# Weighting both halves of the first states with C in one product, and adding the residual inside the output projection

## The chip, the cores and the metric

The kernel runs on one core of a Trainium2 chip. The metric is the device time of one execution in microseconds; "the time" of a kernel is the median of several runs. Five engines work from queues of their own: TensorE (PE in the profile, with its weight loads as PEld), VectorE (DVE), ScalarE (ACT), GpSimd (POOL) and SyncE (SP), which issues nearly all the DMAs.

## The reference, cut to what matters

One decoder layer on x of shape (4, 512, 256): a two-layer state-space (Mamba-like) block, cross attention, and a mixture-of-experts block, each with a residual. Only the first matters here:

```
x = x + ssm(layernorm(x))          # ssm keeps a residual stream of its own, cur
for l in 0, 1:
    cur = cur + block(rmsnorm(cur))

block: xb, z   = split(in_w @ .)              xb = silu(conv(xb))
       delta, B, C = projections of xb        delta = softplus(...)
       dA[e,n,t] = exp(delta[e,t] * A[e,n])   mi[e,n,t] = delta[e,t] * B[n,t] * xb[e,t]
       v[t] = 0.6 * v[t-1] + mi[t]            h[t] = dA[t] * h[t-1] + v[t]      (16 states n, 512 channels e)
       y[e,t] = sum_n h[e,n,t] * C[n,t] + D[e] * xb[e,t]
       return out_w @ (y * silu(z))
```

So each of the 4 x 2 = 8 (layer, batch) steps ends in an output projection of 512 tokens x 256 features, whose result is added to `cur`; after layer 1 the layer's own input x is added as well.

## The kernel before, in words

The stage runs over eight steps s = (l, b): layer 0 with batches 0 to 3, then layer 1. A step has eight pairs (lines 652 and on): a pair is one block of 128 channels (e, four of them) and two of its four groups q of 32 channels. The 128 partitions of a tile hold 32 channels times four states. A pair has state slots n = 0 to 3. For n = 1, 2, 3 one whole unit each treats both groups in tiles of 128 x (2 x 512). For n = 0, the first states, there are two half units of 128 x 512, one for each group j. The five units of a pair come in an order written by hand (`TURNS`, line 59; f is a whole unit, h a half): "ffhfh" for the first four pairs, "fhfhf" for three, "hfhff" for the last. In all there are 192 whole and 128 half units. A unit's number within the step is its slot, 0 to 39.

A whole unit: POOL makes `m` = dx * B (`driven`, line 693), two whole units ahead; DVE scans it with 0.6 into `v` (L729, in PSUM) and then with the decay into `h` (L738); POOL weights `h` with C in place (`weighted`, L751); PE sums over the states into the PSUM tile `y` with the matrix `joined` (`summed`, L765). A half unit has no `m` and no first scan: PE filters by a banded matrix into the PSUM tile `vf` (`filtered`, L711, 20 small products, placed two units ahead; the pool holds one `vf`), and DVE scans that with the decay into `hh` (L726). POOL weights each half when it has been scanned. The two halves of a pair go to PE together:

```
hc = weighted(u, h)
...
pending.append((u, hc[:, 0, :], hc[:, 1, :]) if n > 0 else (u, half, hc[:, 0, :]))
```

Decays are made by ScalarE with Exp (`decayed`, L684), three groups ahead, into four tiles. Once the units of a channel block are done, `finished` (L778) multiplies `y` with the gate `z` on DVE. After the last block of a step, it starts `projected`, a generator that advances one piece at each whole unit of the next step. Its first piece runs at slot 3 of that step, the second at slot 5, the end at slot 6. A piece computes 256 tokens with eight matmuls into a PSUM tile `po` of 128 x 2 x 256 (L798), from the pool "mm" of two buffers, which all products of the background share:

```
for t in range(0, TB, 2):
    po = ps.tile([P, 2, D], F32, tag="mm", name="po")
    ...
    yield
    cur = xs[:, b, t : t + 2, :]
    nc.vector.tensor_tensor(cur, cur, po, ALU.add)
    if l == NL - 1:
        nc.gpsimd.tensor_tensor(cur, cur, xt[:, t : t + 2, :], ALU.add)
```

`xs` in SBUF holds the residual stream `cur` of all four batches. Layer 1 loads x again into `xt` by a DMA on SP at the head of its projection (L793). The last step's projection isn't made here but in the attention stage (L1343), by code of its own. So seven projections pass through `projected`: four of layer 0, three of layer 1.

Beside this, a background generator, `prologue`, prepares the next step (norm, transposes `pt` L474, `xnT` L477, input products `pp` L383, convolution `pc` L490, softplus through `sum` L572, DMAs to and from HBM), with the current step's gates in between (product L383, Silu L465). It rests while a projection is under way, except at slots 1 to 4. [...] At slot 2 PE has `vf` for slot 4, the first product of a new `y` (L761) and the sums held back; at slot 3 the first `po`; at slot 4 a gate product `pp` and a sum; at slot 5 the second `po` and then `vf` for slot 7.

Of the kernel before, what the change touches and what calls it, by code (L numbers as in the profile page):

```python
# [10 lines left out]
F32 = mybir.dt.float32  # L11
I32 = mybir.dt.int32
AF = mybir.ActivationFunctionType
ALU = mybir.AluOpType
# [3 lines left out]
P = 128  # L18
B, L, D = 4, 512, 256
KD = D // P  # L20
TB = L // P
NL = 2
# [45 lines left out]
def decoder_layer(  # L68
# [26 lines left out]
    nc = tc.nc  # L95
# [5 lines left out]
    xs = const.tile([P, B, TB, D], F32, name="xs")  # L101

    ident = const.tile([P, P], F32, name="ident")
# [106 lines left out]
    with ExitStack() as ph:  # L210
# [7 lines left out]
        pre6 = ph.enter_context(tc.tile_pool(name="ssm_pre6", bufs=6))  # L218
        ring2 = ph.enter_context(tc.tile_pool(name="ssm_ring2", bufs=2))
        ring3 = ph.enter_context(tc.tile_pool(name="ssm_ring3", bufs=3))  # L220
        ps_beta = ph.enter_context(tc.tile_pool(name="ssm_ps_beta", bufs=1, space=PSUM))
        ps_v = ph.enter_context(tc.tile_pool(name="ssm_ps_v", bufs=1, space=PSUM))
        ps_vf = ph.enter_context(tc.tile_pool(name="ssm_ps_vf", bufs=1, space=PSUM))
# [430 lines left out]
        for i in range(len(pairs)):  # L654
            ns, js = iter(range(1, SQ)), iter(((0,), (1,)))
# [42 lines left out]
        left = []  # L698

        filtering = {}  # L700

        def filtered(u):

# [16 lines left out]
        def scanned(u):  # L720
            i, n, js = units[u]
            dA = decaying[i, n][:, js[0] : js[-1] + 1, :]
            if n == 0:
                v = filtering.pop(u)
                h = ring3.tile([P, L], F32, name="hh")
                nc.vector.tensor_tensor_scan(h, dA[:, 0, :], v, 0.0, ALU.mult, ALU.add)  # L726
                return h.unsqueeze(1)
            v = ps_v.tile([P, 2, L], F32, name="v")
            nc.vector.tensor_tensor_scan(  # L729
                v.rearrange("p n t -> p (n t)"),  # L730
                beta.rearrange("p n t -> p (n t)"),
                entering.pop(u).rearrange("p n t -> p (n t)"),
                0.0,
                ALU.mult,
                ALU.add,
            )
            h = ring3.tile([P, 2, L], F32, name="h")
            nc.vector.tensor_tensor_scan(  # L738
                h.rearrange("p n t -> p (n t)"),
                dA.rearrange("p n t -> p (n t)"),  # L740
                v.rearrange("p n t -> p (n t)"),
                0.0,
                ALU.mult,
                ALU.add,
            )
            return h

        def weighted(u, h):
            i, n, js = units[u]
            Cs = made[pairs[i][0]][3][1]  # L750
            nc.gpsimd.tensor_tensor(h, h, Cs[n].unsqueeze(1).to_broadcast([P, len(js), L]), ALU.mult)  # L751
            return h

        def summed(u, *hcs):
# [32 lines left out]
        def projected(s, z):  # L787

            l, b = s
            outw = weights[l][5][0]  # L790
            if l == NL - 1:
                xt = pre1.tile([P, TB, D], F32, tag="w", name="xt")
                nc.sync.dma_start(xt, blocks(x[b]))  # L793
            for t in range(0, TB, 2):
                po = ps.tile([P, 2, D], F32, tag="mm", name="po")
                for i in range(2):
                    for k in range(NE):
                        nc.tensor.matmul(  # L798
                            po[:, i, :],
                            z[k // 2][:, k % 2, (t + i) * P : (t + i + 1) * P],  # L800
                            outw[:, k, :],
                            start=(k == 0),
                            stop=(k == NE - 1),
                        )
                yield
                cur = xs[:, b, t : t + 2, :]
                nc.vector.tensor_tensor(cur, cur, po, ALU.add)
                if l == NL - 1:
                    nc.gpsimd.tensor_tensor(cur, cur, xt[:, t : t + 2, :], ALU.add)


        DOUBLE = (8, 23, 38), (8, 13, 18, 23, 30, 33, 38)
# [23 lines left out]
        pending = []  # L836
# [74 lines left out]
        for u, (i, n, js) in enumerate(units):  # L911
            s, e, q = pairs[i]
            if u % 16 == 15 and empty < NX * ROWS + SPARE * P:
                empty = emptied(empty)
            if u % 16 == 7:
                next(fillers, None)
            if u % per == 0 and (e, q) == (0, 0):
                k = steps.index(s)
                if k == 0:
                    background = chained(background, prologue(*steps[1], s))  # L920
                    foreground = None
                else:
                    for _ in background:
                        pass
                    if s == (1, 0):
                        load_others(1)
                    if k + 1 < len(steps):
                        background, foreground = prologue(*steps[k + 1], s), None
                    else:
                        background, foreground = kept_from(), gates(s)  # L930

                fetching = k > 0 and k + 1 < len(steps) and steps[k + 1][0] == 0
                if fetching:
                    next(background)
                slot = 0
            if s == (1, 0) and slot == 10:
                load_last(1)
            if u in groups and groups.index(u) + LEAD < len(groups):
                later = groups[groups.index(u) + LEAD]
                i2 = units[later][0]  # L940
                if later % per == 0 and i2 + 1 < len(pairs):
                    while pairs[i2 + 1] not in stored:
                        next(background)
                    copied(i2 + 1)
                owed.append(later)
            between = units[u - 1][1:] == (0, (0,))
            while owed and not between and (n > 0 or 0 in js):
                decayed(owed.pop())
            if n > 0 and wholes.index(u) + AHEAD < len(wholes):
                driven(wholes[wholes.index(u) + AHEAD])  # L950
            gating = 3 if TURNS[i // 2 * 2 % len(TURNS)][1] == "h" else 2
            if u % per == gating and q == 0 and u > per:
                finished(*pairs[i - 1][:2])
            h = scanned(u)
            if projections:

                if n > 0 and next(projections[0], s) is s:
                    projections.pop()
            elif slot > 1 and foreground is not None:
                if next(foreground, s) is s:  # L960
                    foreground = None
            early = n == 0 and js == (0,)
            hc = weighted(u, h)

            def filters():
                if u + 2 < len(units) and units[u + 2][1] == 0:
                    s2, e2 = pairs[units[u + 2][0]][:2]
                    while (s2, e2 // 2) not in ready:
                        next(background)
                    filtered(u + 2)  # L970

            def sums():

                while pending and not 0 < slot % (2 * per) < gating:
                    summed(*pending.pop(0))

            if early:
                filters()
                sums()
                half = hc[:, 0, :]  # L980
            else:
                if n > 0:
                    filters()
                if 0 < slot <= 4 or not projections and foreground is None and not (fetching and slot == 0):
                    held = next(background, None)
                    if held is None and not projections and (
                        n > 0 and (k == 0 and slot < 20 or k == len(steps) - 1 or units[(u + 1) % len(units)][1] > 0) or slot in DOUBLE[k < len(steps) - 1]
                    ):
                        next(background, None)
                if n == 0:  # L990
                    filters()
                sums()
                pending.append((u, hc[:, 0, :], hc[:, 1, :]) if n > 0 else (u, half, hc[:, 0, :]))
            if k + 1 < len(steps) and slot in (36, 38):
                spread(steps[k + 1], 0 if slot == 36 else 3)
            if slot == 36 and k + 1 < len(steps):
                bands = banded()
            if slot >= 36 and k + 1 < len(steps):
                for _ in range(2):
                    next(bands, None)  # L1000
            slot += 1
# [263 lines left out]
    with ExitStack() as ph:  # L1265
# [20 lines left out]
        for i in range(2):  # L1286

            t = wp.tile([P, TB, P], F32, name=f"tops{i}")
# [10 lines left out]
        xt = ring.tile([P, TB, D], F32, tag="wide", name="xt")  # L1299
# [74 lines left out]
        n = B * NG * 8  # L1374
        for s in range(-LEAD, n + 2):
            u, k = divmod(s, 8)
            kb, hp = divmod(k, 2)
            b, g = divmod(u, NG)
# [340 lines left out]
```

## Time and profile before

| | us |
|---|---|
| median of 3 runs (1794.42 to 1799.02) | 1794.95 |
| the profiled execution, its own time | 1799.32 |
| its span, first to last instruction | 1797.6 |
| mean granted TensorE clock | 0.935 |

The groups of instructions that the change removes, merges or adds to (by line, with shapes kept apart; xN is the count, then the busy time in us and the mean ns of one):

| line, engine, what | count | busy us | mean ns |
|---|---|---|---|
| L751 POOL, `h` times C, 128x1024 | 192 | 452.6 | 2357 |
| L751 POOL, `hh` times C, 128x512 | 128 | 163.0 | 1274 |
| L807 DVE, `xs` plus `po`, 128x512 | 14 | 9.6 | 683 |
| L809 POOL, `xs` plus `xt`, 128x512 | 6 | 7.6 | 1269 |
| L798 PE, `po`, 128x256 | 224 | 52.1 | 386 |
| L484 ACT, copy from PSUM, 128x512 | 32 | 18.6 | 581 |

L798 counts two instructions for each matmul of this data type (112 matmuls). Matmuls overlap, so the mean of one is longer than its pace: 16 in a row take 3.72 us. The page gives each engine's busy share, and its busy tenths in 40 slices of 45 us; the state-space stage is slices 2 to 27. The waits view says who waited for whom. The chain of waits goes back from the last instruction, at each step to what released it. A timeline row holds the start, the duration, the engine, line, operation and tiles, and in square brackets the idle time before it with what ended it.

### The profile page before, as it was taken

How to read it: one execution, taken by the hardware profiler on the slowest of the kernel's cores; microseconds unless marked ns; L12 is line 12 of the kernel's file. 1: busy time of each engine (PE TensorE's matmuls, PEld its weight loads, DVE VectorE, ACT ScalarE, POOL GpSimd, SP SyncE). 2: the span in 40 equal slices, each digit the busy share in tenths (PEclk: the TensorE clock that was granted, in tenths of full speed). 3: DMA queues.
4: the chain of work that ended last, by engine and by line, in shares of the span. 5: the costliest groups of instructions: out<-in, count | busy, mean ns of one | idle time of the engine just before them, and what ended most of it. 6: DMA issues, size and time to landing. Idle time of an engine off the chain costs nothing.

```text
span 1797.6 us, 28225 instructions
## 1 busy us (share of the span) xinstructions
PE 1569.9 (87%) x10682; PEld 737.0 (41%) x10682; DVE 1379.8 (77%) x1252; ACT 1027.8 (57%) x1613; POOL 1242.0 (69%) x781
## 2 busy tenths in 40 slices
PE   7779789879879879879879978987999999889998
PEld 3333344334334334334424324433233333466665
DVE  1498899989999999999999998995567676532223
ACT  3758767747876866866776865541444444412221
POOL 4588999989989999999999999992000202245540
PEclk9889999989999889989979988996999999999999
DMA  2543543553553653634553443533310100442214
GB/s 64 142 106 92 138 109 98 121 112 95 132 131 78 151 132 99 155 100 101 140 133 83 138 114 99 161 109 120 106 59 24 59 1 24 145 119 66 65 59 152
DMA packets 122991, 185.71 MB, mean 103 GB/s; under 512 B 19464, under 2 KB 58248, under 8 KB 122856
## 3 DMA queue, kind: packets, MB, share of 16 engines
q1 hardware_dynamic: 117576, 169.45, 36.0%
q0 software_dynamic: 5280, 14.46, 2.6%
q8 instruction: 85, 1.39, 0.3%
q14 instruction: 50, 0.41, 0.1%
HBM read 124.38 MB, written 59.46 MB: 102 GB/s over the span
## 4 chain that ended last, share of the span: by engine, by line
PE 60%; DVE 16%; ACT 11%; issue 7%; POOL 3%; DMA 3%; SPq 0%; DVEq 0%; POOLq 0%; ACTq 0%
DVE v L729 7%; PE y L765 7%; PE pc L490 6%; PE sT L1415 6%; PE pp L383 5%; PE vf L711 5%; DVE h L738 4%; PE pu L1569 4%; PE pw L1592 4%; PE o L1328 3%; ACT decay L684 3%; PE sum L572 3%; PE sc L1415 3%; PE po L798 2%; PE y L761 2%
## 5 line engine op out<-in xcount | busy, mean ns | idle before, releaser
L751 POOL TENSOR_TENSOR h<-h,Cs 128x1024 f32<-128x1024 f32 x192 | 452.6, 2357 | 49.6 <-DVE h L738 39.9
L693 POOL TENSOR_TENSOR m<-dxs,Bs 128x1024 f32<-128x1024 f32 x192 | 452.8, 2359 | 16.1 <-DMA deltas<-wide 16.1
L738 DVE TENSOR_TENSOR_SCAN h<-decay,v 128x1024 f32<-128x1024 f32 x192 | 439.0, 2286 | 17.0 <-DVE v L729 0.5
L729 DVE TENSOR_TENSOR_SCAN v<-beta,m 128x1024 f32<-128x1024 f32 x192 | 437.9, 2281 | 14.8 <-POOL m L693 9.8
L684 ACT ACTIVATE decay<-deltas,scaleA 128x511 f32<-128x511 f32 x512 | 332.0, 712 | 58.5 <-DVE h L738 57.4
L711 PE MATMUL vf<-band,dxT 106*32 106x102 f32 (+1 forms) x5120 | 184.5, 269 | 87.3 <-DVE hh L726 86.5
L765 PE MATMUL y<-h,joined 128*32 128x512 f32 x768 | 210.3, 643 | 30.3 <-POOL h L751 30.0
L1421 DVE TENSOR_REDUCE tops<-sc 128x2 f32<-128x1024 f32 x128 | 156.3, 1225 | 96.5 <-PE sc L1415 96.3
L711 PEld LDWEIGHTS vf<-band,dxT 106*32 106x32 f32 (+1 forms) x5120 | 145.6, 117 | 165.6 <-issue 109.8
L1426 ACT ACTIVATE at<-sT 128x1024 f32<-128x1024 f32 x128 | 128.8, 1024 | 140.6 <-PE sc L1415 109.0
L726 DVE TENSOR_TENSOR_SCAN hh<-decay,vf 128x512 f32<-128x512 f32 x128 | 154.1, 1204 | 31.0 <-PE vf L711 31.0
L751 POOL TENSOR_TENSOR hh<-hh,Cs 128x512 f32<-128x512 f32 x128 | 163.0, 1274 | 13.8 <-DVE hh L726 10.2
L113 POOL TENSOR_TENSOR rstd<-ve,neghalf 128x4 f32<-128x4 f32 x12 | 12.3, 1027 | 204.3 <-DVE ve L111 204.3
L1415 PE MATMUL sc<-kpad,qpad 32*128 32x512 f32 x512 | 146.1, 668 | 7.2 <-ACT at L1426 4.8
L1415 PE MATMUL sT<-q,kpad 32*128 32x512 f32 x512 | 139.4, 658 | 3.3 <-DVE q L1320 3.3
L383 PE MATMUL pp<-xnT,inw 128*128 128x512 f32 x256 | 124.0, 622 | 4.9 <-ACT z L649 3.4
L490 PE MATMUL pc<-xpad,taps 128*128 128x512 f32 x256 | 118.9, 604 | 0.0
L765 PEld LDWEIGHTS y<-h,joined 128*32 128x32 f32 x768 | 35.5, 115 | 141.2 <-issue 67.2
L1601 POOL DMA_INDIRECT rows_out<-yg,target x39 | 40.0, 1027 | 77.1 <-DVE xgT L1562 69.1
L1196 POOL DMA_INDIRECT rows_in<-row,at x32 | 31.8, 994 | 80.8 <-DVE stat L1209 39.6
L684 ACT ACT_TABLE_LOAD x62 | 79.5, 1283 | 4.6 <-DMA deltas<-wide 3.5
L1585 DVE COPY hgT<-pf 128x512 f32<-128x512 f32 x39 | 27.0, 692 | 68.3 <-PE pf L1583 68.3
(252 smaller groups left out, 2301.3 us busy)
## 6 DMA issues: line engine op xcount, KB each, us to landing
dxs<-wide SPq DMA_DIRECT2D x256, 128.0 KB, 2.7
deltas<-wide SPq DMA_DIRECT2D x256, 128.0 KB, 3.1
rows_in<-nothing SPq DMA_DIRECT2D x17, 1028.0 KB, 8.9
Cs<-rows SPq DMA_DIRECT2D x128, 64.0 KB, 3.3
wide<-w SPq DMA_DIRECT2D x16, 512.0 KB, 2.8
wide<-ln SPq DMA_DIRECT2D x16, 512.0 KB, 3.8
Bs<-rows SPq DMA_DIRECT2D x32, 192.0 KB, 3.8
xt<-in_x_dram SPq DMA_DIRECT2D x8, 512.0 KB, 7.2
```

What stands on the lines that cost most here:

```text
L383: nc.tensor.matmul(pp, weights[l][1][half][:, k, m * P : (m + 1) * P], xnT[:, k, :], start=(k == 0), stop=(k == KD - 1),)
L490: nc.tensor.matmul(pcs[j], taps[:, e, k, :], xpads[j][:, k : k + L], start=(k == 0), stop=(k == KC - 1),)
L684: nc.scalar.activation(dA[:, j, 1:], copies[i][0][:, j, 1:], AF.Exp, scale=weights[s[0]][6][:, e, q + j, n : n + 1])
L693: nc.gpsimd.tensor_tensor(m, copies[i][1], Bs[:, n - 1, :].unsqueeze(1).to_broadcast([P, 2, L]), ALU.mult)
L711: nc.tensor.matmul(v[r * QP : (r + 1) * QP, CHUNKS[c] : CHUNKS[c + 1]], made[s][5][e // 2][:k, c, first : first + QP], band[:k, c, r, : CH ...
L726: nc.vector.tensor_tensor_scan(h, dA[:, 0, :], v, 0.0, ALU.mult, ALU.add)
L729: nc.vector.tensor_tensor_scan(v.rearrange("p n t -> p (n t)"), beta.rearrange("p n t -> p (n t)"), entering.pop(u).rearrange("p n t -> p ...
L738: nc.vector.tensor_tensor_scan(h.rearrange("p n t -> p (n t)"), dA.rearrange("p n t -> p (n t)"), v.rearrange("p n t -> p (n t)"), 0.0, AL ...
L751: nc.gpsimd.tensor_tensor(h, h, Cs[n].unsqueeze(1).to_broadcast([P, len(js), L]), ALU.mult)
L765: nc.tensor.matmul(ys[s, e][(q + j) * QP : (q + j + 1) * QP, :], joined, hcs[j], start=False, stop=(u % per == per - 1),)
L1415: nc.tensor.matmul(o, l, m, start=True, stop=True)
L1421: nc.vector.tensor_reduce(top[:, t2, 2 * h : 2 * h + 2, HD : HD + 1], sc, AX.X, ALU.max, negate=True)
```

## The change

It has two parts. The tiles of the two halves become one: the first half unit takes a tile of 128 x 2 x 512, each half scans into its own half of it, and POOL weights both with one product after the second half. These tiles and those of the whole units come from one pool of four buffers, in place of two pools of three. And in the output projection PE multiplies the identity with `cur` (and, in layer 1, with `xt` too) into the same PSUM tile ahead of the eight products, so that `po` holds the new residual stream; ScalarE copies it to `xs`. DVE's add and POOL's add are gone.

```diff
+        ring4 = ph.enter_context(tc.tile_pool(name="ssm_ring4", bufs=4))
...
             if n == 0:
                 v = filtering.pop(u)
-                h = ring3.tile([P, L], F32, name="hh")
-                nc.vector.tensor_tensor_scan(h, dA[:, 0, :], v, 0.0, ALU.mult, ALU.add)
-                return h.unsqueeze(1)
+                if 0 in js:
+                    halves[i] = ring4.tile([P, 2, L], F32, tag="h", name="hh")
+                h = halves[i]
+                nc.vector.tensor_tensor_scan(h[:, js[0], :], dA[:, 0, :], v, 0.0, ALU.mult, ALU.add)
+                return h
...
-            h = ring3.tile([P, 2, L], F32, name="h")
+            h = ring4.tile([P, 2, L], F32, tag="h", name="h")
...
-            nc.gpsimd.tensor_tensor(h, h, Cs[n].unsqueeze(1).to_broadcast([P, len(js), L]), ALU.mult)
+            nc.gpsimd.tensor_tensor(h, h, Cs[n].unsqueeze(1).to_broadcast([P, 2, L]), ALU.mult)
...
+                cur = xs[:, b, t : t + 2, :]
+
+                more = (cur, xt[:, t : t + 2, :]) if l == NL - 1 else (cur,)
                 for i in range(2):
+                    for j, x_of in enumerate(more):
+                        nc.tensor.matmul(po[:, i, :], ident, x_of[:, i, :], start=(j == 0), stop=False)
                     for k in range(NE):
                         nc.tensor.matmul(
                             po[:, i, :],
                             z[k // 2][:, k % 2, (t + i) * P : (t + i + 1) * P],
                             outw[:, k, :],
-                            start=(k == 0),
+                            start=False,
                             stop=(k == NE - 1),
                         )
                 yield
-                cur = xs[:, b, t : t + 2, :]
-                nc.vector.tensor_tensor(cur, cur, po, ALU.add)
-                if l == NL - 1:
-                    nc.gpsimd.tensor_tensor(cur, cur, xt[:, t : t + 2, :], ALU.add)
+                nc.scalar.copy(cur, po)
...
-            hc = weighted(u, h)
+            hc = h if early else weighted(u, h)
...
-                half = hc[:, 0, :]
...
-                pending.append((u, hc[:, 0, :], hc[:, 1, :]) if n > 0 else (u, half, hc[:, 0, :]))
+                pending.append((u, hc[:, 0, :], hc[:, 1, :]))
```

In each engine's program the other instructions keep their order: the copies stand on ScalarE after the decays of slots 5 and 6, the second ahead of the gate's table load; the joined product stands on POOL where the second half's stood.

More of the change, by code (lines that the diff above doesn't have):

```diff
@@ L700, in decoder_layer @@
         filtering = {}
+        halves = {}
         def filtered(u):
```

## The prediction

> **What bounds the kernel now.** I began with the page: busy shares, then the 40 slices. The state-space stage (first scan at 64.4 us, last gate product ending near 1220) is what the change touches; the 577 us behind it only move along.
>
> ```profile
> PE 1569.9 (87%) x10682; PEld 737.0 (41%) x10682; DVE 1379.8 (77%) x1252; ACT 1027.8 (57%) x1613; POOL 1242.0 (69%) x781
> ...
> DVE  1498899989999999999999998995567676532223
> ...
> POOL 4588999989989999999999999992000202245540
> ```
>
> Over 64.4 to 1220.1 the table of windows gives DVE 1072.7 busy of 1155.7 us, POOL 1080.3, PE 981.1, ACT 797.6. DVE and POOL are 93% busy, so a shorter DVE or POOL list looks like a gain. Whether it is one depends on what each engine waits for where the change acts. The DVE waits of the whole span:
>
> ```profile
> DVE hh L726 <- PE vf L711: 31.0, 27, 5.4
> ...
> DVE z L778 <- PE y L765: 8.9, 4, 3.6
> ...
> DVE xs L807 <- PE po L798: 7.2, 9, 1.7
> ```
>
> No scan waits for POOL after the start (the only such wait, 9.8 us, is the first scan): POOL runs two units ahead with `m`, and its weighting is read by PE alone. DVE's stalls come from PE. So I read the chain of waits around one projection, that of (1,0), and DVE beside it:
>
> ```profile
> 797.90 1.22 DVE hh L726
> ...
> 799.26 1.94 PE vf L711 x40
> 801.20 2.01 PE y L761 x2
> 803.21 2.43 PE y L765 x8
> 805.64 3.65 PE po L798 x16
> 809.29 1.72 PE pp L383 x4
> 811.01 0.98 PE y L765 x4
> 811.99 3.65 PE po L798 x16
> 815.64 1.02 PE vf L711 x40
> ```
>
> ```profile
> 809.33 0.68 DVE L807 TENSOR_TENSOR xs<-xs,po 128x512 f32<-128x512 f32 x1
> ...
> 815.68 0.69 DVE L807 TENSOR_TENSOR xs<-xs,po 128x512 f32<-128x512 f32 x1 [1.06 <-PE po L798]
> 816.79 1.22 DVE L726 TENSOR_TENSOR_SCAN hh<-decay,vf 128x512 f32<-128x512 f32 x1 [0.43 <-PE vf L711]
> ```
>
> The reader is to see that PE runs without a gap from one half scan (797.90) to the end of the filter `vf` that the next pair's half scan (816.79) needs, that both halves of the projection `po` lie in that run, and that DVE twice waits for it. DVE's own work from 797.90 to 816.79 is one half unit 1.13, a whole unit 4.58, a half 1.12, and two wholes at 4.6: 16.0 us, 17.2 with both `xs` adds, against 18.9 taken. In all seven projections (chunks at 240, 385, 523, 666, 806, 946, 1088 us) that half scan shows the same 0.43 us wait for `vf`. **Here PE sets the time, not DVE.**
>
> **The change, part by part.**
>
> *DVE's 14 adds (L807)*: 9.6 us busy at 683 ns plus 7.2 us waits leave DVE. All 14 lie in these seven stretches, ahead of a half scan that waits for PE; without them it is reached sooner and waits longer. Worth 0 where PE is late; 16.8 us if PE were not (rival 1). What is late next is `vf`.
>
> *TensorE gets the identity products*: per half of a projection 2 matmuls of 128x256 for layer 0, 4 for layer 1. Four projections of layer 0 and three of layer 1 pass here (the eighth has its own code): 4x2x2 + 3x2x4 = 40. A chunk of 8 matmuls (16 instructions) takes 3.72 us, so one costs 0.465 us; a layer-0 chunk grows by 0.93, a layer-1 chunk by 1.86 us. Both chunks stand before `vf` on the gapless run, so the half scan comes 1.86 us later (layer 0), 3.72 us later (layer 1). The exception is the third: there PE waits 1.24 us for POOL's weighting between the chunks; POOL has shed a 1.28 us half product ahead of it, so that wait goes, and the delay is about 2 x 0.93 - 1.24 = 0.6. Sum: 3 x 1.86 + 0.6 + 3 x 3.72 = 17.3 us. Below nothing this can't go: nothing leaves PE. Above, PE could wait for data. The x tile's DMA is issued at 796.37 and lands in 6.7 us, about 803.5, while PE needs it at about 806.1: 2.6 us of slack, cost 0; its place on SP's queue is unchanged. Were it some 3 us later than that, it would cost the excess, three times.
>
> *ScalarE gets 14 copies*: a copy of 128x512 out of PSUM takes 0.58 us (L484, L616), so 8.1 us, on an engine 69% busy in the stage. The places matter more. The first copy is queued behind decays and waits for the first chunk; the second chunk reuses its PSUM buffer, but the gate product (1.72) and a sum (0.98) stand between on PE, so 0.6 us of copy is hidden. Behind the waiting copies stand decays (issued three groups ahead; DVE shows no wait for one: some 5 us of cover) and the gate:
>
> ```profile
> 810.80 1.28 ACT L465 ACT_TABLE_LOAD   x1
> 814.81 0.60 ACT L465 ACTIVATE z<-pp 128x512 f32<-128x512 f32 x1 [2.73 <-PE po L798]
> 815.43 1.28 ACT L684 ACT_TABLE_LOAD   x1
> 816.72 1.33 ACT L684 ACTIVATE decay<-deltas,scaleA 128x511 f32<-128x511 f32 x2
> 818.13 1.27 ACT L477 ACTIVATE xnT<-pt,nw 128x512 f32<-128x512 f32 x2
> ```
>
> Now table load and gate run while PE still does the second chunk. After the change the second copy, which must wait for that chunk's end (call it E, 815.64 here), stands ahead of both. From E: copy 0.7, load 1.28, gate 0.6, load 1.28, decays 1.3, `xnT` 1.27 = E + 6.4. PE wants `xnT` for `pp` at E + 5.6 today (821.25). Also the transposes need the gate's PSUM buffer: E + 2.6 against E + 1.9. So `pp` starts some 0.9 us later, and DVE's next gate product (833.15) has only 0.1 us of cover, as PE's last sum ends at 833.08. Five steps have this form (the third hangs on POOL, the seventh has other background): 5 x 0.8 = 4 us. Lower bound 0, if PE finds other work; upper 5 x 1.5. A page says worse: the Trainium skill, *ScalarE: Activation LUTs*, section "What ACT_TABLE_LOAD costs", counts about 1.38 us of drain on top of every 1.28 us load. With two loads behind the copy that would be 2.8 us more per step, 14 in all; but in the row above decays start 0.01 us after the load's end, so I take the row.
>
> *POOL*: 128 half products at 1274 ns become 64 whole ones at 2357: 163.0 - 150.9 = 12.1 us less; the six adds L809 take 7.6 more away. 19.7 us leave an engine DVE does not wait for: taken as 0. The price is order. Both halves' product now stands behind the second half scan and takes 2.36 where 1.27 stood, so POOL is 1.1 us late for the next weighting; the next first half, which now asks nothing of POOL, gives it back. PE's sum of that pair comes 1.1 us later. Of 64 such places PE waits for `h` from POOL in 13 and idles 30 us there; 0 where covered, 1.1 at most: 0 to 13 x 1.1 = 14 us. I take 0, since in the stretches read the sum follows several us behind the product (an `hh` sum at 832.0 for a product ended at 827.1).
>
> *Buffers*: `h` and `hh` had three each, now share four. Per pair four tiles are taken, so each gets its buffer back after one pair (about 17 us); the first half's scan must wait for PE's sum of the pair before, which follows within two units. Taken as 0; a late sum would cost its lateness.
>
> *What needs the residual later*: the next layer's squares run on ScalarE, behind the copy; the queries' statistics on DVE come a step later. 0.
>
> **Sum.** 17.3 + 4 - 0 = 21.3 us. The profiled execution took 1799.32 us (span 1797.6 and 1.7 around it), 4.4 above the median of the three runs, 1794.95. So 1820.6 for an execution like the profiled one, and about **1816 us** as median.
>
> **Rivals.**
>
> 1. *DVE is the bound, PE's additions fill its holes*: 1795 - 16.8 = 1778 us. For it: PE waits 86.5 us for half scans, and a rule. The Trainium skill, *Perfetto Trace Analysis*, section "Identifying the Most-Contended Engine", has occupancy name the engine for Vector, Scalar and GpSimd, and holds matmul busy time a bad measure: by it DVE and POOL at 93% are what to shorten, giving this sum. Against: PE's holes lie before 799.26 (7.33 us just ahead of it), not between chunk and scan; there the rows give the opposite sign, +17.3. It decides only if each projection has over 1.86 (3.72) us of PE slack.
> 2. *Half and half*: the stretches lose PE's delay, but DVE, with 16.8 us less work, catches up in later PE-bound places (waits of 0.74 and 2.42 us for `vf` recur each step): 21.3 - 7 x 3 = 0 at best, about 1795. Against: those waits shift with PE too.
> 3. *Slower still*: POOL's late whole product reaches PE's sums at all 13 places: 1816 + 14 = 1830.
> 4. *The scalar knock-on is hidden*: 17.3 alone, 1812.
>
> **How the numbers follow.** Forecast 0.57; rival 4 0.22; rival 3 0.09; rival 2 0.07; rival 1 0.05. A difference of 0.3% (5.4 us) is about what measurement can tell from no change. Forecast and rivals 3 and 4 are slower, 0.88, and a third of rival 2 too: 0.90; the rest of rival 2, 0.05, within; rival 1, faster, 0.05. The range: from 1804 (half the PE delay absorbed) to 1826 (the knock-on's upper bound, a few of POOL's places).
>
> **What would show it.** In the new profile, at each projection: `po` chunks of 4.65 and 5.58 us instead of 3.72; DVE waiting for `vf` at the half scan behind it for about 4 to 5 us (layer 0) and 6.6 us (layer 1), so this wait's total near 65 us instead of 31; the gate table load behind the copy; `xs` gone from DVE's list, POOL near 1222 us busy with more idle time. The stage should end near 1241 instead of 1220 and the 577 us behind stay. I am wrong if the half scan behind the second chunk comes no later, if the DVE wait for `z` does not appear, or if PE waits for ScalarE's copy or the x tile.

## The result and the profile after

| | before | after |
|---|---|---|
| median, executions taken side by side | 1796.99 us (4 runs, 1794.42 to 1800.57) | 1818.74 us (4 runs, 1813.01 to 1819.54) |
| ratio after / before, 95% interval | | 1.0104 [1.0085, 1.0123] |
| the profiled execution | 1799.32 us, span 1797.6 | 1813.01 us, span 1811.3 |
| end of the last `z` product | 1220.78 us | 1232.53 us |
| from there to the end of the span | 576.8 us | 578.8 us |

The changed kernel is slower: by the ratio on record, which has the interval, 1.04%, 18.7 us of 1797 (15 to 22). The two medians lie 21.75 us apart (1.21%), within that interval. The two profiled executions lie only 13.7 us apart: that of after is the lowest of its four times, that of before lies near the top of its own. So places are read from the profiles, and totals in us are the ratio's difference from 1 times the time of before. Ratios are of undisturbed executions; a single one (7290 us, in run e3 below) is left out.

The busy line of the changed kernel's page, to be set against the one shown of before:

```profile
PE 1586.4 (88%) x10762; PEld 752.7 (42%) x10762; DVE 1373.4 (76%) x1238; ACT 1034.6 (57%) x1627; POOL 1224.6 (68%) x711
```

DVE has lost 14 instructions and 6.4 us, POOL 70 and 17.4 us; PE has gained 80 (40 products) and 16.5 us of merged busy time. Two engines got lighter, the kernel slower. The waits of DVE (who waited for whom, us in total, times, longest):

```profile
DVE hh L730 <- PE vf L713: 47.2, 25, 7.2
...
DVE z L782 <- PE y L769: 8.4, 9, 2.5
```

The half scans wait 47.2 us for the filter `vf` where they waited 31.0; `xs` has gone from the list. The same projection as in the prediction, that of (1,0), in time order on PE (start, duration, instruction):

```profile
801.28 1.94 PE L713 MATMUL vf<-band,dxT 104*32 104x104 f32 x40 [7.32 <-DVE hh L730]
...
806.85 0.70 PE L805 MATMUL po<-xs,ident 128*128 128x256 f32 x2
807.38 0.59 PE L805 MATMUL po<-xt,ident 128*128 128x256 f32 x2
807.82 1.89 PE L807 MATMUL po<-outw,z 128*128 128x256 f32 x8
809.54 0.59 PE L805 MATMUL po<-xs,ident 128*128 128x256 f32 x2
809.98 0.59 PE L805 MATMUL po<-xt,ident 128*128 128x256 f32 x2
810.41 1.89 PE L807 MATMUL po<-outw,z 128*128 128x256 f32 x8
812.13 1.88 PE L384 MATMUL pp<-xnT,inw 128*128 128x512 f32 x4
...
814.93 0.70 PE L805 MATMUL po<-xs,ident 128*128 128x256 f32 x2
...
820.30 1.09 PE L713 MATMUL vf<-band,dxT 104*32 104x104 f32 x40
```

A chunk now runs from 806.85 to 812.13, 5.28 us from start to next start, where it took 3.56 us, measured in the same way (805.57 to 809.13): 1.72 us more for four identity products. The second takes 5.37. PE is gapless here as before, from 801.28 on, and its longer run ends in `vf`. DVE and ScalarE in the same stretch:

```profile
813.96 2.29 DVE L742 TENSOR_TENSOR_SCAN h<-decay,v 128x1024 f32<-128x1024 f32 x1
821.56 1.22 DVE L730 TENSOR_TENSOR_SCAN hh<-decay,vf 128x512 f32<-128x512 f32 x1 [5.31 <-PE vf L713]
```

```profile
812.33 0.59 ACT L815 COPY xs<-po 128x512 f32<-128x512 f32 x1 [4.03 <-PE po L807]
...
820.41 0.59 ACT L815 COPY xs<-po 128x512 f32<-128x512 f32 x1 [6.26 <-PE po L807]
821.01 1.28 ACT L466 ACT_TABLE_LOAD   x1
822.31 0.60 ACT L466 ACTIVATE z<-pp 128x512 f32<-128x512 f32 x1
822.92 1.28 ACT L685 ACT_TABLE_LOAD   x1
```

The half scan of slot 7 had 0.43 us of idle time before it and now has 5.31: DVE finishes its shorter list earlier and stands still. On ScalarE the table load and the gate stand behind the second copy, as foreseen, and the load begins 0.7 us after PE has gone on to `vf`.

### The profile page after: what moved, and what is told of

Its sections match the earlier page's. It is cut to its first block, busy times and chain, and to the rows that moved or that the text cites. A ratio compares the mean times of both kernels' runs of the same rounds, so it can differ in the third digit from the quotient of the medians.

```text
span 1811.3 us, 28308 instructions
## 1 busy us (share of the span) xinstructions
PE 1586.4 (88%) x10762; PEld 752.7 (42%) x10762; DVE 1373.4 (76%) x1238; ACT 1034.6 (57%) x1627; POOL 1224.6 (68%) x711
## 4 chain that ended last, share of the span: by engine, by line
PE 61%; DVE 14%; ACT 12%; issue 7%; DMA 3%; POOL 2%; SPq 1%; DVEq 0%; POOLq 0%; ACTq 0%
PE y L769 7%; PE pc L491 6%; DVE v L733 6%; PE sT L1421 6%; PE pp L384 5%; PE vf L713 5%; ACT decay L685 4%; PE pw L1598 4%; PE pu L1575 4%; DVE h L742 4%; PE sum L573 3%; PE o L1334 3%; PE sc L1421 3%; PE po L807 2%; PE y L765 2%
## 5 line engine op out<-in xcount | busy, mean ns | idle before, releaser
L769 PE MATMUL y<-h,joined 128*32 128x512 f32 x768 | 204.4, 626 | 21.5 <-POOL h L755 21.3
L730 DVE TENSOR_TENSOR_SCAN hh<-decay,vf 128x512 f32<-128x512 f32 x128 | 154.3, 1205 | 53.2 <-PE vf L713 47.2
L755 POOL TENSOR_TENSOR hh<-hh,Cs 128x1024 f32<-128x1024 f32 x64 | 151.1, 2360 | 4.2 <-DVE hh L730 4.2
L1421 PE MATMUL sc<-kpad,qpad 32*128 32x512 f32 x512 | 145.8, 667 | 7.9 <-ACT at L1432 4.8
L1421 PE MATMUL sT<-q,kpad 32*128 32x512 f32 x512 | 138.5, 652 | 3.3 <-DVE q L1326 3.3
L384 PEld LDWEIGHTS pp<-xnT,inw 128*128 128x128 f32 x256 | 47.8, 195 | 75.7 <-issue 55.4
```

Source lines behind the costliest of these rows:

```text
L384: nc.tensor.matmul(pp, weights[l][1][half][:, k, m * P : (m + 1) * P], xnT[:, k, :], start=(k == 0), stop=(k == KD - 1),)
L730: nc.vector.tensor_tensor_scan(h[:, js[0], :], dA[:, 0, :], v, 0.0, ALU.mult, ALU.add)
L769: nc.tensor.matmul(ys[s, e][(q + j) * QP : (q + j + 1) * QP, :], joined, hcs[j], start=False, stop=(u % per == per - 1),)
L1421: nc.tensor.matmul(o, l, m, start=True, stop=True)
```

## The experiments

All ratios are against the kernel before, run on the same chip in the same session. The "stretch" is read from the profiles: from the start of the half scan at slot 4 to the start of that at slot 7 (803.61 to 816.79 in the projection of (1,0)), summed over the seven projections, less the same sum of before. In after it is +15.2 us. Single profiles scatter: that of before is of a long execution (1799.32 against 1794.95 us), and e1, with the same TensorE work in these stretches, reads -4.1. So differences of some 4 us in this column say little.

| run | ratio [95%] | stretch, us |
|---|---|---|
| after | 1.0104 [1.0085, 1.0123] | +15.2 |
| e1 halves joined, projection as before | 1.0018 [1.0009, 1.0028] | -4.1 |
| e2 projection changed, halves as before | 1.0103 [1.0083, 1.0123] | +15.3 |
| e3 as e2, VectorE copies | 1.0091 [1.0073, 1.0110] | +13.1 |
| e4 ScalarE copies, nothing added | 1.0000 [0.9990, 1.0009] | -0.9 |
| e5 as e2, first identity products early | 1.0079 [1.0061, 1.0097] | +7.7 |
| e6 as e2, `vf` ahead of the second chunk | 1.0148 [1.0126, 1.0169] | -16.9 |
| e7 before, 4 throwaway products | 1.0010 [1.0000, 1.0020] | -3.5 |
| e8 as e2, identity products twice | 1.0209 [1.0195, 1.0223] | +31.9 |
| e9 before, 7 throwaway products | 0.9986 [0.9976, 0.9997] | -6.8 |
| e10 after, 7 throwaway products | 1.0041 [1.0027, 1.0055] | +5.9 |
| e11 as e5, 5 or 6 throwaway products | 1.0028 [1.0017, 1.0039] | +1.5 |
| e12 as e4, 7 throwaway products | 0.9921 [0.9899, 0.9943] | -6.7 |

### Which half of the change costs: e1 and e2

e1 is the kernel before with the joined halves alone (the new tiles, the pool of four, one product by C); e2 is the kernel before with the projection alone:

```diff
+                    for j, x_of in enumerate(more):
+                        nc.tensor.matmul(po[:, i, :], ident, x_of[:, i, :], start=(j == 0), stop=False)
...
-                nc.vector.tensor_tensor(cur, cur, po, ALU.add)
-                if l == NL - 1:
-                    nc.gpsimd.tensor_tensor(cur, cur, xt[:, t : t + 2, :], ALU.add)
+                nc.scalar.copy(cur, po)
```

> Only the first part of the change: both halves of the first states in one tile and one product on POOL; the projection as before. Theory (PE's run of work sets the time in the projection stretches, POOL's time is covered): ratio 1.000, within 0.2%; POOL 12 us less busy, its idle time up by as much. Rival 'POOL and DVE are the bound': 12 us of POOL saved show, 0.994 or so. Rival 'the late whole product stalls PE': 1.002 to 1.008, with PE's waits for POOL up.

> Only the second part: identity products in PE, copies on ScalarE; the halves weighted apart as before. Theory: it carries the whole loss, ratio 1.0104 (1.008 to 1.012), +18 us. If the two parts share the loss, 1.005. Rival 'DVE is the bound': 0.991.

The projection part alone gives 1.0103, the whole change 1.0104. The joined halves alone cost 3 us (1.0018, interval 1.6 to 5), which the sum of the two parts does not show; the intervals allow both; POOL was 9.7 us less busy in e1 and the kernel did not gain from it. Where e1's 3 us lie was not found: its stretches are even shorter than those of before.

### What in the projection costs: e3, e4 and e8

e3 lets VectorE copy, e4 leaves the identity products out, e8 issues them twice:

```diff
e3, against e2
-                nc.scalar.copy(cur, po)
+                nc.vector.tensor_copy(cur, po)
e4, against e2
-                    for j, x_of in enumerate(more):
-                        nc.tensor.matmul(po[:, i, :], ident, x_of[:, i, :], start=(j == 0), stop=False)
e8, against e2
-                    for j, x_of in enumerate(more):
-                        nc.tensor.matmul(po[:, i, :], ident, x_of[:, i, :], start=(j == 0), stop=False)
+                    for r in range(2):
+                        for j, x_of in enumerate(more):
+                            nc.tensor.matmul(
+                                po[:, i, :], ident, x_of[:, i, :], start=(j == 0), stop=(r == 0 and j == len(more) - 1)
+                            )
```

> As the run before it, but DVE copies po to xs (where it added before) in place of ScalarE. Theory: DVE has time to spare ahead of the half scan, so DVE's work is the same as before and PE's 18.6 us alone are tested: +14 to +17 us, ratio 1.008 to 1.0095. If the loss comes from the copies on ScalarE, the time falls back to about 1.000. If ScalarE's copies were a gain in themselves, it is slower than the run before it by 8 us or more.

> Leaves out the residual: no identity products and no adds, ScalarE copies the bare projection to xs (the residual stream and x are not added). So DVE's 14 adds and POOL's six are gone and PE's work is as before. Theory: DVE waits for the filter instead, and PE's chain is as long as before: ratio 0.998 to 1.003 (the knock-on through the gate's table load costs up to 4 us, DVE's lost adds give at most 2 back). Rival 'DVE is the bound and loses 16.8 us': 0.991.

> The residual part alone, with every identity product issued twice (the second pass starts the sum afresh, so the result is unchanged): 40 more products at 0.465 us = 18.6 us more TensorE work at the same seven places, and no other engine gets more or less. Theory (TensorE's amount of work ahead of the half scan sets these stretches, one for one): about 18 us above the residual alone, ratio 1.020, DVE's waits for vf about 18 us longer than its 57.6. Rival A (much of the residual's cost is a fixed one, the new order of copy, table load and gate): the second dose costs little, ratio 1.010 to 1.013. Rival B (a part of the first dose was hidden in slack that is now used up): more than the first dose, over 1.022.

e8 is the clearest run. One dose of 40 products costs 1.03%, two cost 2.09%: 18.5 us (15 to 22) and 37.5 us (35 to 40) of 1795, against 18.6 us of TensorE work per dose (40 x 0.465). The waits of DVE, in e2, e8 and e4:

```profile
DVE hh L726 <- PE vf L711: 57.6, 28, 7.2
```

```profile
DVE hh L726 <- PE vf L711: 75.9, 31, 10.6
```

```profile
DVE hh L726 <- PE vf L711: 43.7, 31, 5.4
```

From e2 to e8 DVE waits 18.3 us more for `vf`, for 18.6 us more of products. So close a match is chance, since this total is 57.6 in e2 and 47.2 in after, with the same products; but the cost of two doses is twice that of one within the intervals, and a fixed cost (rival A) is out. Step by step it is not one for one. From the start of the half scan at slot 2 to the same point of the next step, the four steps with a projection of layer 0 took 564.6 us in before, 566.0 in e2 and 576.4 in e8: 1.4 us for the first dose and 10.3 for the second, where each adds 7.4 us of products. The first two steps with a projection of layer 1 took 282.5, 289.3 and 296.2: 6.8 us for each dose. But before, e1, e4 and e7, all without identity products, read 562.6 to 565.9 us in the four steps, so whether layer 0 had slack that the first dose used up (rival B) stays open.

Who copies matters little (e3 and e2: 1.0091 and 1.0103, intervals that overlap). e4 takes the adds away from DVE and POOL and gives PE nothing: ratio 1.0000, -0.9 us in the stretches, and DVE waits 43.7 us for `vf` instead of 31.0. What DVE no longer does there, it waits. One reservation on e4: its stage ends 2.8 us later than that of before in the profiles, and the part behind it takes 568.5 us instead of 576.8. That part varies (last section) and runs on other data in e4, which leaves the residual out, so its ratio cannot tell a gain of some 5 us from none. The 16.8 us of rival 1 are out.

### Taking the products off the path: e5 and e6

e5 makes the first chunk's identity products at slot 1, in PE's idle time (and loads x a slot earlier for it). e6 places `vf` for slot 7 ahead of the second chunk:

```diff
e5, against e2
+            if k > 0 and slot == 1:
+                begun[steps[k - 1]][1] = residual(steps[k - 1], 0)
e6, against e2
+            moved = n > 0 and bool(projections)
+            if moved:
+                filters()
             if projections:
...
-                if n > 0:
+                if n > 0 and not moved:
                     filters()
```

> The residual in PE and the copies on ScalarE as in the second part of the change alone (1.0103), but the identity products of each projection's first half are issued at slot 1, where PE idles 7.3 us before the chain starts, as one product of 128x512 for each source; x is loaded one slot earlier so that it is there. Those of the second half stay in the chain. Theory (PE work on the gapless run is what costs): 4 x 0.93 + 3 x 1.86 = 9.3 us of 18.6 leave the run, ratio 1.0045 to 1.006. If the loss were due to the copies, the buffers or PE work in general, wherever it stands, 1.010 stays.

> The second part of the change alone (1.0103), with the filter for the half scan moved ahead of the projection's second half on PE at slot 5. Theory: DVE no longer waits at that half scan, but PE has as much work up to the next gate product at slot 12, whose last sum then comes as late: the wait moves from vf to z, ratio 1.008 to 1.0105. Rival 'only the order ahead of the half scan costs': the loss goes, ratio 1.000 or below.

e5: the stretches got back 7.6 of e2's 15.3 us, about the half that was moved. The ratio got back only 4.3 us (1.0079) where 9.3 us of products had moved, less than expected. In its profile, measured from slot 2 to slot 2 as above, the two steps of layer 1 are back at 282.4 us, all that e2 had lost there; the four of layer 0, at 569.8, are longer than e2's 566.0. e11 asks after these. e6 is a miss, and a useful one. The half scan of slot 7 now comes with next to no wait, and the one of slot 9 waits instead; first DVE's row there, then PE's:

```profile
835.75 1.22 DVE L726 TENSOR_TENSOR_SCAN hh<-decay,vf 128x512 f32<-128x512 f32 x1 [4.36 <-ACT decay L684]
```

```profile
833.11 0.66 PE L474 MATMUL pt<-ident,xn 128*128 128x128 f32 x4 [1.02 <-ACT z L465]
...
834.58 1.05 PE L711 MATMUL vf<-band,dxT 104*32 104x104 f32 x32
```

The releaser named for DVE is a decay, but `vf` ends at 835.63, 0.1 us before the scan: that is the wait. The filter for slot 9 stands behind the second chunk, a sum and transposes, and these transposes wait 1.02 us for the gate on ScalarE, which is queued behind the copy. Measured from slot 4 to slot 9, the seven stretches grew by 10.0 us although those to slot 7 shrank by 16.9. So the new order changed which scan pays for the TensorE work and uncovered the knock-on through ScalarE. It cost more besides (1.0148 against e2's 1.0103): from slot 9 to slot 37 the steps grew by another 14.2 us, most of it in waits of DVE for `z`, 2.0 us in six steps and 4.1 in the last, where before has 0.1 in five. So a part of the wait moved to `z`, as expected. Why the sum is larger than e2's was not tried.

### TensorE's clock in the same stretch: e7, e9 and e10

The rows ahead of the first chunk (`vf`, the new `y`, the sums) took 6.38 us in before and 5.57 in after, for the same instructions. The table of windows gives the granted clock (the column ahead of the last two), for before, after and e9 in turn:

```profile
799.26:805.64 6.38, 6.38 (x51) 2.63 (x51) 6.28 (x4) 3.62 (x8) 6.30 (x6) 0.60 0.11 35
```

```profile
801.28:806.85 5.57, 5.57 (x51) 2.44 (x51) 5.47 (x4) 2.82 (x6) 5.15 (x5) 0.68 0.11 36
```

```profile
790.92:794.83 3.91, 3.91 (x50) 1.53 (x50) 3.81 (x2) 1.71 (x4) 3.83 (x5) 1.00 0.17 57
```

In before and after PE has idled for 7.3 us just ahead. The Trainium skill, *TensorE: Matmul & The Clock Gate*, section "What's actually happening", says that the array falls to half its clock after an idle window of about 3.4 us and comes back after as much sustained work, the window running freely. In before's trace the clock falls to half at 794.13, 2.2 us after PE's last product and so before a whole such time had been idle, and is whole again from 804.38, 5.1 us after PE resumed:

```profile
799.26:804.38 5.12, 5.12 (x46) 2.44 (x48) 5.02 (x3) 2.36 (x6) 5.04 (x5) 0.50 0.14 42
804.38:805.64 1.26, 1.26 (x7) 0.19 (x3) 1.26 (x2) 1.26 (x4) 1.26 (x2) 1.00 0.02 7
```

So 0.60 is the mean of a half and a whole part. e7 and e9 fill the idle time of the kernel before with four and seven products whose result is thrown away; e10 does it to the changed kernel:

```diff
+            if k > 0 and slot == 1:
+                warm = bank("warm")
+                for _ in range(7):
+                    nc.tensor.matmul(
+                        warm, ident, xs[:, steps[k - 1][1], 0:2, :].rearrange("p t d -> p (t d)"), start=True, stop=True
+                    )
```

> The kernel before with four throwaway identity products of 128x512 on PE at slot 1 of steps 1 to 7 (their result is not used), in the 7.3 us idle time before the filter of slot 4. Asks whether the low granted clock right behind that idle time (0.60 over 6.3 us) is part of what sets the time. If the clock follows PE's activity and PE is the bound: filter, first product of y and sums run at full pace, up to 2.4 us in each of seven steps, ratio 0.991 to 0.996. If either is not so: 1.000, or up to 1.004 where the products run late into the filter.

> The kernel before, with seven throwaway identity products of 128x512 (some 6.5 us of TensorE work) in the idle time ahead of the filter for slot 4, steps 1 to 7, so that TensorE has next to no idle time there. If the low granted clock of the rows that follow comes from the idle time before, vf takes 1.1 to 1.5 us instead of 1.94 and the y sums 1.9 instead of 2.4, half scan 7 comes 1 to 2 us sooner in each of seven steps: ratio 0.993 to 0.997. If the clock does not follow so short an activity, or the gain is given back at the next wait: 0.999 to 1.001. If the products are too slow and run into vf: over 1.002.

> The changed kernel with the seven throwaway products of e9 ahead of the filter for slot 4. Before the change the half scan waited only 0.43 us there, so a faster TensorE could win little (e9: 0.9986); after the change it waits 3.5 to 7.2 us, so every us that the rows between the two half scans lose at the low granted clock can be won. From the windows of these stretches (clock 0.50 to 0.71, the rows ahead of the projection 5.6 us instead of about 4.2) 1.2 to 2 us in each of seven steps: 8 to 14 us below the changed kernel's 1.0104, ratio 1.003 to 1.006. If the low clock in these rows is not a cost (rival), or is given back at the next wait, only what e9 won is seen: 1.008 to 1.010.

e7 was a miss: four products (3.70 us) left another 3.70 us idle, and `y` and its sums were slow again (2.07 and 2.13 us, where e9 has 1.12 and 1.91). In e9, seven products leave 1.12 us:

```profile
783.52 6.28 PE L958 MATMUL warm<-xs,ident 128*128 128x512 f32 x14
790.92 1.09 PE L711 MATMUL vf<-band,dxT 104*32 104x104 f32 x40 [1.12 <-DVE hh L726]
791.94 1.12 PE L761 MATMUL y<-xb,diagD 128*128 128x512 f32 x2
```

Full pace from the first row on (`vf` 1.09 us instead of 1.94). That is worth only 0.14% to the kernel before, less than expected. Its half scan had only 0.43 us of waiting to lose, and the 14 adds waited 7.2 us in all (3.2 in e9). And what is won can be given back at the next wait: in the steps of (1,0) and (1,1) the stretch fell by 1.7 and 1.3 us, and the gate product on DVE, which had waited 0.12 us for PE's last sum, now waits 1.75 and 1.39. In (1,0):

```profile
824.72 0.69 DVE L778 TENSOR_TENSOR z<-y,z 128x512 f32<-128x512 f32 x1 [1.75 <-PE y L765]
```

In the changed kernel the scan waits 3.5 to 7.2 us, and there the same products take 11 us off (1.0104 to 1.0041), as expected in all; in the profile the gain lies in the two steps of layer 1 (289.1 to 282.7 us), not in the four of layer 0 (566.3 and 566.0). The two ratios together say what the change costs with a warm TensorE: 1.0041 / 0.9986 - 1 = 0.55%, 10 us (some 7 to 13), where it cost 18.7. A likely reason, not tried by itself: in e9 four of the seven half scans start without a wait, so PE had slack to lose there.

### Both remedies, and the other bound: e11 and e12

e11 is e5 with five (layer 1) or six throwaway products ahead of the early identity products; e12 is e4 with the seven of e9.

> The early identity products of e5, with five or six throwaway ones ahead of them, so that TensorE is busy from slot 1 to the filter for slot 4. e5 took half of the identity products off the run that sets the time and won only 4 of the 9 us. If the rest was lost to the low granted clock behind the idle time, it comes back here: the second chunk's identity products (9.3 us) less 8 to 14 us of clock, ratio 0.997 to 1.002. If e5's rest was lost to something else (the shared PSUM buffers held longer, other places), ratio 1.005 to 1.008.

> The kernel before, with ScalarE copying po to xs (the residual stream and x are not added at all, so the layer's residual is left out), and with the seven throwaway products of e9. With TensorE sped up by e9, the half scan no longer waits for vf in five of seven steps, so VectorE, not TensorE, should set these stretches; its two adds (0.68 us each, and 1.7 us of waits for po in all before) are then on the path. Theory: what was worth 0.0% in e4 is now worth up to 7 x 1.4 = 9.6 us, capped by what TensorE then asks: ratio 0.994 to 0.997 against e9's 0.9986. Rival: the adds are still worth nothing, 0.998 to 0.999.

e11 gives 1.0028, between its two expectations. The throwaway products took 9 us off e5 (14 to 5), about as much as the 11 us that they took off after; so the low clock cost e5 as well. In the profiles 3.5 us of this lie in the four steps of layer 0 (569.8 to 566.3), where e5 had missed its gain, and next to nothing in the two of layer 1; the rest is not placed, and what it costs that the PSUM buffer of the early products is held from slot 1 on was not tried by itself. No complete version with the residual on TensorE beat the kernel before. The only complete kernel ahead of it is e9, by 0.14%, under what the 0.3% of the prediction calls measurable. e12 asked whether DVE's adds become worth something once PE is fast. The ratio says yes, 0.9921 against 0.9986, 12 us, more than the 9.6 that the adds could give. The profiles carry only a part: the stretches are as long as e9's (-6.7 and -6.8), the stage ends only 3.3 us earlier than e9's, and 5.3 us lie in the part behind the stage, which runs on other data because the residual is missing. The two steps of layer 1 took 275.7 us, 6.6 less than e9's, the four of layer 0 3.3 us more. So the worth of the adds on a warm TensorE stays open, between 3 and 12 us.

## Why the prediction was right, and where it was not

The forecast was 21.3 us more, about 1816 us. Measured were 1818.74 us, 21.75 more by the medians and 18.7 (15 to 22) by the ratio.

**PE, not DVE, sets these stretches**: right, and shown by e4 (adds away, products not there: nothing), e2 (products there: all of it) and e8 (twice the products, twice the cost). One reading is loose: PE has no gap from 799.26 on, not from 797.90, where the half scan starts whose end lets `vf` begin; the chain of the two is as long as stated.

**17.3 us for the identity products**: +15.2 us in after's stretches; 18.5 us by the ratio of e2, and 19 for e8's second dose. The price of 0.465 us each was right within a few per cent (four cost 1.72 us in a row, 0.43 each). By step, the stretch grew by 1.8, 1.9, 0.4, 0.9, 2.8, 2.8 and 4.5 us; predicted were 1.86, 1.86, 0.6, 1.86 and three times 3.72. A part of the shortfall is the granted clock ahead of the chunk, higher than in before's profile (5.57 against 6.38 us in the fifth). The prediction took that clock as fixed; it differs from one execution to the next. A further 3.5 us came back between slots 9 and 37, where the last half scan waits 1.0 to 2.4 us for `vf` in six steps of before and 0.46 in after. e1, which keeps the adds, has the same 0.46, and e7, with the work of before there, 0.9 to 1.4; so this is at least in part before's long execution and no proof of rival 2's catching up.

**4 us for the knock-on through ScalarE**: mis-sized; the order of events was as foreseen. The gate product had no cover of 0.1 us, as the prediction reads its rows: in before it already waited 0.12 us for that sum in five steps. The wait is 0.35 us in after (predicted 0.8 for each of the five):

```profile
838.21 0.69 DVE L782 TENSOR_TENSOR z<-y,z 128x512 f32<-128x512 f32 x1 [0.35 <-PE y L769]
```

PE's `pp` came 5.97 us after the chunk's end instead of 5.61, so 0.4 us later, not 0.9. With the same wait shorter in the third step (0.67 us, was 1.37) and in the seventh (2.18, was 3.59), the seven waits sum to 4.6 us against 5.6: net nothing. Such waits come also with the copies but no products (e4: 0.47 us in four of the five steps) and without copies (e1: 0.7 in two), so what makes them is not separated. Rival 4, 17.3 us alone, was nearer to what the parts did; the interval (15 to 22 us) excludes neither. That the sum of 21.3 lies so near the measured time is in part luck: the knock-on gave nothing in all, and in the pair of profiles the four steps of layer 0 grew by 1.7 us where 6.2 of products were forecast; the next two, of layer 1, came near (6.6 of 7.4).

**POOL and DVE relieved, worth 0**: right. POOL's 17.4 us became idle time. The late whole product of rival 3 did not show: PE's waits for `h` from POOL fell from 30.0 us to 21.3. e1's +3 us is the one sign that joining the halves is not quite free.

**x tile, buffers**: PE never waited for the x tile; the two layer-1 chunks start back to back behind the sums, and PE's only wait for a copy of ScalarE is one of 1.3 us.

**Rivals 1 and 2** fell with the measured slowdown, and rival 1's bound with e4. The total of the waits for `vf` was foretold as 65 us and is 47.2 (50.7 with one that the trace puts down to POOL): too high for after, though e2, with the same products, reached 57.6.

## What to carry to other kernels

Before work is moved from a busy engine to an idler one, look at the very stretch where it lands: here the "less busy" TensorE ran without a gap there, so 18.6 us of products cost some 18.5 us (15 to 22), and what was taken from two engines at 93% bought nothing (9.7 us of POOL in e1; 9.6 us of DVE and 7.6 of POOL in e4). Test such a claim by leaving the work out on one side (e4) and by doubling it on the other (e8), and distrust a new order (e6) that makes one wait vanish until the next scan behind it has been read. If the landing stretch begins after an idle time of TensorE, look at its granted clock first.

## What the runs showed of the hardware

**An idle time of 3.7 us already costs TensorE its clock, one of 1.1 us does not.** After 7.3 us of idle time the 50 instructions ahead of the chunk took 5.6 to 6.4 us; after 1.1 us of it (e9) 3.91; after 3.7 us (e7) `y` took 2.07 us, where it takes 1.12 at full pace. In after and before the slow part had a different length for the same instructions, so executions differ by up to 0.8 us at each such place.

**The steps come in lengths some 3.4 us apart.** The step that holds the projection of (1,0), from its slot 2 to that of the next (797.90 to 937.89 in before), took 136.5 us in e12; 139.8 to 140.2 in eight profiles (before, e1, e4, e5, e7, e9, e10, e11); 143.2 to 143.4 in after, e2 and e3; 146.5 and 146.8 in e6 and e8; and nothing between. So a change of 1 or 2 us in such a step can be worth 0 or 3.4: e9 shortened its stretch by 1.7 us and the step by 0.2, e5 moved 1.86 us of products away and the step fell by 3.5 from e2's. In the traces all changes of the granted clock lie on marks 3.413 us apart; in before it falls at 794.13 and again at 934.08, 41 such times later. That the steps fall in with these marks is a guess that no run tried.

**The part behind the stage varies by itself.** From the last `z` product to the end it took 568.5 to 578.8 us over the 14 profiles, though none of the edits touches it. It differs also between runs on the same data (569.9 in e7, 576.8 in before). The longest share of it lies between the last score maximum (L1421 of before) and the first product of the expert part (L1569), 63.1 to 69.0 us, and most of the rest ahead of that maximum. What makes it so was not tried. It is one reason not to read differences of a few us from a single pair of profiles. That the pair of before and after gave 13.7 us where the ratio gives 18.7 is another matter: there this part differs by only 2.0 us, and the shortfall lies in the stage, which ends 11.8 us later.
